# Layer 1's table, layer 2's scores and the shared outputs: an order of work changed at three places of a four-layer kernel

## The chip, the core and the metric

The kernel runs on one core of a Trainium2 chip. The core has TensorE (PE, matrix products and turns through an identity), VectorE (DVE), ScalarE (ACT), GpSimd (POOL, which here also issues the indirect DMAs) and SyncE (SP, which issues plain DMAs). Each engine takes its own instructions strictly in the order of the program's list for it and waits for the others by semaphores. The metric is the time of one execution on the device, in microseconds; shown is the median of three runs.

## What is computed

2048 tokens (8 sequences of 256) of 512 numbers pass four layers. Each layer adds a gated attention-like part and a gated feed-forward part to the tokens x, both of the normalised tokens. The change touches the seam of layers 1 and 2 and layer 2 with layer 3's attention beside it. Cut to that:

```python
# layer 1, feed-forward: 64 experts, 8 chosen for each token, and a shared one
out1 = experts(x, topk_idx, topk_w) + (silu(x @ sh_gate) * (x @ sh_up)) @ sh_down
x = x + tanh(g_ffn[1]) * out1

# layer 2, attention over channels, for each sequence
scaled = einsum('bsd,bse->bde', q, k) / sqrt(512)      # q = layernorm(x), k = v = ctx
out = einsum('bde,bse->bsd', softmax(scaled, axis=1), v)

# layer 2, feed-forward
out2 = gelu(x @ proj1.T + b1) @ proj2.T + b2

# layer 3, attention: a recurrence over the 256 tokens of a sequence, channel by channel
def step(carry, kv_t):                                 # k = layernorm(x), v = ctx
    aa, bb, pp = carry
    q = max(pp, u + kt)
    y_t = (exp(pp - q) * aa + exp(u + kt - q) * vt) / (exp(pp - q) * bb + exp(u + kt - q))
    q2 = max(pp + w, kt)
    return (exp(pp+w-q2) * aa + exp(kt-q2) * vt, exp(pp+w-q2) * bb + exp(kt-q2), q2), y_t

# layer 3, feed-forward: 8 experts, 2 chosen for each token, and a shared one
```

## The kernel before

All numbers are float32. The tokens stay in 16 tiles `xt[0..15]` of 128 tokens; four tiles make a block of 512 tokens (`NB` = 4 blocks), two a sequence. The program is a list written by hand in Python, and a list scheduler orders each engine's instructions by their place in the program and by a model of when their inputs are ready. `behind(one, other, reason)` adds a pure order constraint: `one` stands after `other` in the list. `with tc.high_priority` moves work forward in it. Where work of two kinds is to be interleaved, one of them is a Python generator, and the other calls `step` or `next`, which places the generator's next piece at this point. Matrix products go to four PSUM banks `mm`, turns to two banks `tr`, and two banks `ac` take the rest.

**Layer 1.** `attend1(blk, step)` (from L833) computes the attention of a block, and each of its calls of `step(n)` does two things (L1145): it advances `work()`, which routes the pairs of tiles q = 0 to 6 one after the other through `route1(q)` (from L969), and it issues up to `n` of the pending table writes. With `hurry` both are done twice; the second sequence of the last block is attended with `hurry` (L861). A table write (L950) is an indirect DMA from POOL that puts 128 choices, one from each token of a tile, into their experts' rows of a table in device memory; there are 16 to a route, 128 in all, and each may be told to come after a given product of PE. `route1(q)` normalises (statistics and `ve` on DVE, `rstd` on POOL at L166, `xn` on DVE), turns and scores its two tiles, chooses experts on DVE, and finds the weight of each choice with 16 small DVE operations `hit` (L1064).

After the attention the last route, q = 7, runs at high priority beside the shared expert of blocks 0 to 2. `shared1(blk)` (L1087) has five pieces: the products shg, shu and shr, with a multiplication `shT` on DVE in two parts at L1110, and two pieces of down products shd (16 PE passes for a block), each of which is scaled and added to its tiles of `xt` on DVE at L221. The loop at L1162 takes a piece of `shared1`, writes up to three pending choices behind the piece's last product, and takes a piece of `route1(7)`; in the eighth round that gives `order`, the experts by how many tokens they have, from which SP loads expert weights. All 16 choices of route 7 are written without such a tie. Then the table is read back (`rows`, L1177, one indirect DMA after all 128 writes), turned by PE into `who_ps` (L1193), and copied as `who` (DVE) and `share` (ACT). `who` is what the experts' tiles gather their tokens by (`xg`, L1213), on POOL; `tr_xg` turns what was gathered. The experts add their results by indirect DMA to two copies of the output in device memory, `acc`.

Last, after the experts, come the shared expert of block 3 (L1336), and `combine` (L1344), which loads the two copies of a tile (`more`, through eight buffers `t2`, by SP) and adds them to `xt` on DVE, L1352.

**Layer 2.** `back()` combines and normalises block 0 by pairs of tiles (L1725), and so lets the scores of the first sequence begin. `xattn2(blk)` (L1369) has for each of two sequences four score products `s` of PE, each followed by a maximum (L1385), an exponential `E` on ACT (L1387), a reciprocal and a scaling of `vs` (L1391); then four outputs `o`. The keys `kxvs` are loaded by SP, into a pool `bp` of five buffers that also holds one of the two `E` and, for layer 3, the turned tokens `xnT_a` and the exponents `ex`. `ready2` places the norm for the feed-forward part, `ffn2`, beside the second sequence; `ffn2` (L1436) has four quarters of four first products `h2p` (a gelu on ACT behind each) and four second ones `o2f` (a DVE addition behind each). Its weights `p` come by SP through seven buffers `wp`.

**Layer 3 beside it.** `tail(blk)` (L1681) is layer 3's attention and routing of a block: one piece for the norm, 12 for each of four groups of 128 channels (scans `pp`, `aa`, `bb`, and `q`, `ex`, `num`, `den` and a reciprocal on DVE; differences and products on POOL; an exponential on ACT), then four pauses, four pieces that turn and add the result, and nine of routing, of which the last ones issue eight table writes from POOL (L1669): 66 in all. It is advanced by `step(n, behind)` (L1699) of the back part; `held` puts the first DVE operation of a piece behind the given instruction. `tail(0)` and `tail(1)` are spread over `xattn2(2)`, `ffn2(1)` and over `xattn2(3)`, `ffn2(2)`; `tail(2)` over `ffn2(3)`; `last(blk, i)` (L1709) flushes what is left with `step(1000)` after the first `o2f` of the last quarter.

## Time and profile before

| | |
|---|---|
| time, three runs | 2718.54, 2718.95, 2723.67 us; median 2718.95 |
| the profiled execution | 2704.81 us, of which the span from first to last instruction is 2703.0 |
| PE busy | 2553.9 us, 94% of the span |
| DVE, ACT, POOL busy | 1288.3, 671.9 and 890.6 us (48, 25 and 33%) |
| mean granted TensorE clock | 0.974 |
| DMA | 333.04 MB moved, mean 123 GB/s |

The page gives, besides such totals, the span in 40 equal slices of 67.6 us, with one digit for each, the busy share in tenths (PEclk is the clock that TensorE was granted, in tenths of its full speed):

```profile
PE   7889898999999899999999899898999999999998
DVE  7656575536655622222222641767666674121121
PEclk9999899999999899999999999999999999999999
```

Layer 1's attention ends at 912 us, in the fourteenth slice; its experts run from 984 to 1494; layer 2 begins at 1518, in the 23rd slice, and ends at 2141; from there on it is layer 3's feed-forward part. DVE is nearly full where layer 2 begins and has room while its feed-forward part runs. Further views show single instructions in order of time, what each engine waited for, and busy times of a stretch. In them a line reads: start, duration, engine, line of the program, operation, output<-inputs, shape, number of instructions, and in brackets how long the engine had been idle before and what ended that.

### The profile page before, as it was taken

To read this page: it belongs to the slowest core of one execution; us is meant where nothing else is said; L and a number is where in the kernel's file an instruction comes from. 1 tells how busy PE (TensorE), PEld (TensorE's weight loads), DVE (VectorE), ACT (ScalarE), POOL (GpSimd) and SP (SyncE) were. 2 spreads that over 40 slices of the span, in tenths; PEclk is the share of its full clock that TensorE was granted. 3 is DMA by queue.
4 is the path that set the end of the run, shared out by engine and by line. 5 is a ranking of instruction groups with operands and counts; after the bars stand their busy time and mean duration, and the time that the engine had idled before them with its cause. 6 is when DMAs were issued, how large, how long until landed. Compare 5 with 4: busy or idle time off the path is not lost. (4 is left out here: it accounts for less than half of the span.)

```text
span 2703.0 us, 29475 instructions
## 1 busy us (share of the span) xinstructions
PE 2553.9 (94%) x10253; PEld 1355.1 (50%) x10268; DVE 1288.3 (48%) x3535; ACT 671.9 (25%) x1505; POOL 890.6 (33%) x814
## 2 busy tenths in 40 slices
PE   7889898999999899999999899898999999999998
PEld 3445444455665445555555344344454444455554
DVE  7656575536655622222222641767666674121121
ACT  2534344311111113333333211222223231111110
POOL 1111110112444445656565110333333342333332
PEclk9999899999999899999999999999999999999999
DMA  5000000112200259999997721132121211888884
GB/s 214 9 16 24 20 36 4 33 36 63 64 25 25 59 175 237 246 242 246 243 241 169 224 113 64 38 110 61 61 91 67 106 16 47 278 276 270 288 278 113
DMA packets 96187, 333.04 MB, mean 123 GB/s; under 512 B 20608, under 2 KB 23041, under 8 KB 88098
## 3 DMA queue, kind: packets, MB, share of 16 engines
q0 software_dynamic: 45856, 156.51, 23.0%
q1 hardware_dynamic: 47154, 170.34, 18.6%
q10 hardware_dynamic: 3024, 4.25, 0.5%
q8 instruction: 84, 1.38, 0.2%
q14 instruction: 69, 0.57, 0.1%
HBM read 280.46 MB, written 64.91 MB: 128 GB/s over the span
## 5 line engine op out<-in xcount | busy, mean ns | idle before, releaser
L210 PE MATMUL gu<-w,eb 128*128 128x352 f32 x896 | 285.9, 462 | 0.0
L1293 POOL DMA_INDIRECT acc<-eb,who x112 | 177.5, 1585 | 175.5 <-DVE eb L102 148.3
L210 PE MATMUL h2p<-xnT_f,p 128*128 128x512 f32 x512 | 228.0, 601 | 3.0 <-ACT xnT_f L104 3.0
L210 PE MATMUL o2f<-p,h 128*128 128x512 f32 x512 | 224.8, 593 | 0.0
L210 PEld LDWEIGHTS gu<-w,eb 128*128 128x128 f32 x896 | 162.6, 192 | 73.4 <-issue 2.3
L950 POOL DMA_INDIRECT table<-pay,rowi x128 | 126.1, 985 | 120.6 <-issue 26.1
L539 ACT ACTIVATE pr<-pr,n 128x256 f32<-128x256 f32 x256 | 127.9, 501 | 151.7 <-DVE n L534 148.8
L210 PEld LDWEIGHTS h2p<-xnT_f,p 128*128 128x128 f32 x512 | 97.2, 192 | 120.8 <-issue 115.7
L210 PEld LDWEIGHTS o2f<-p,h 128*128 128x128 f32 x512 | 96.2, 190 | 117.4 <-issue 115.2
L1213 POOL DMA_INDIRECT xg<-xnd,who x112 | 117.2, 1046 | 59.6 <-PE ehp L1240 22.8
L221 DVE SCALAR_TENSOR_TENSOR x<-o2f,tg,x 128x512 f32<-128x512 f32 x64 | 47.0, 739 | 140.7 <-PE o2f L210 140.7
L1768 PE MATMUL g_r<-w,xgT 128*128 128x352 f32 x288 | 111.7, 469 | 0.7 <-ACT xgT L104 0.7
L1768 PE MATMUL u_r<-w,xgT 128*128 128x352 f32 x288 | 108.7, 459 | 0.0
L1284 PE MATMUL ed<-w,eb 128*128 128x512 f32 x224 | 105.7, 594 | 0.9 <-DVE eb L1241 0.9
L102 DVE COPY eb<-ed 128x512 f32<-128x512 f32 x56 | 38.7, 692 | 138.6 <-PE ed L1284 138.6
L1775 DVE SCALAR_TENSOR_TENSOR h_r<-a_r,share,u_r 128x352 f32<-128x352 f32 x36 | 20.9, 581 | 175.9 <-PE u_r L1768 167.4
L1791 PE MATMUL d_r<-w,hT_r 128*128 128x512 f32 (+1 forms) x216 | 104.2, 592 | 0.0
L534 DVE CUSTOM_DVE_ANT_0 pr<-s,mask 128x256 f32<-128x256 f32 x256 | 96.9, 417 | 12.2 <-PE s L514 8.8
L1230 DVE SCALAR_TENSOR_TENSOR eb<-eb,share,gu 128x176 f32<-128x176 f32 x112 | 44.0, 393 | 122.0 <-ACT eb L1229 122.0
L591 POOL TENSOR_TENSOR y<-y,gbo 128x512 f32<-128x512 f32 x16 | 20.4, 1272 | 246.8 <-DVE y L590 239.0
L188 PEld LDWEIGHTS tr_xg<-ident,xg 128*128 128x128 f32 x592 | 68.9, 141 | 63.2 <-issue 49.9
L188 PE MATMUL tr_xg<-ident,xg 128*128 128x128 f32 x592 | 92.7, 280 | 6.4 <-DMA xg<-xnd,who 6.3
(534 smaller groups left out, 4730.5 us busy)
## 6 DMA issues: line engine op xcount, KB each, us to landing
w<-in_w SPq DMA_DIRECT2D x64, 960.0 KB, 7.3
p<-in_p SPq DMA_DIRECT2D x64, 512.0 KB, 5.7
xnd<-xn_f SPq DMA_DIRECT2D x32, 256.0 KB, 3.2
acc<-xnd SPq DMA_DIRECT2D x32, 256.0 KB, 4.9
more<-acc SPq DMA_DIRECT2D x32, 256.0 KB, 4.3
wd<-in_wd SPq DMA_DIRECT2D x64, 96.0 KB, 6.9
ctxTa<-in_ctxT SPq DMA_DIRECT2D x4, 1024.0 KB, 6.0
x<-in_x SPq DMA_DIRECT2D x16, 256.0 KB, 5.9
```

Source lines behind the costliest of these rows:

```text
L188: one = nc.tensor.transpose(ps[:, k, :], src[:, ts(k, P)], ident)
L210: one = nc.tensor.matmul(ps, lhsT[k], rhs[k], start=(k == 0), stop=(k == n - 1))
L221: return nc.vector.scalar_tensor_tensor(xt[i], ps, scale, xt[i], ALU.mult, ALU.add)
L534: one = nc.vector.tensor_tensor_reduce(pr[:, nt, :], ps[r][:, nt, :], mask[:, nt, :], -1.0, -LOW, ALU.add, ALU.min, n16[:, nt, h : h + 1],)
L539: nc.scalar.activation(pr[:, nt, :], pr[:, nt, :], AF.Exp, bias=n16[:, nt, h : h + 1], scale=-1.0, accum_out=s16[:, nt, h : h + 1],)
L950: one = nc.gpsimd.indirect_dma_start(out=table[:, :], out_offset=bass.IndirectOffsetOnAxis(ap=rows, axis=0), in_=choice, in_offset=None, b ...
L1213: nc.gpsimd.indirect_dma_start(out=xg, out_offset=None, in_=xnd[:, :], in_offset=bass.IndirectOffsetOnAxis(ap=who[:, c : c + 1], axis=0), ...
L1230: nc.vector.scalar_tensor_tensor(self.h, self.h, share[:, c : c + 1], gu[:, I1 : 2 * I1], ALU.mult, ALU.mult)
L1284: one = nc.tensor.matmul(ps[n], t.hT[rows, k, :], wd, start=(k == 0), stop=(k == 1))
L1293: nc.gpsimd.indirect_dma_start(out=acc[n][:, :], out_offset=bass.IndirectOffsetOnAxis(ap=who[:, t.c : t.c + 1], axis=0), in_=t.x, in_offse ...
L1768: nc.tensor.matmul(ps[:, 0:I3], xTt[:, k, :], wgu[k][:, g, :], start=(k == 0), stop=(k == KC - 1))
L1791: one = nc.tensor.matmul(ps, hT[:cn, n, :], wd[n][:cn], start=(n == 0), stop=(n == 2))
```

## The change

It is a set of small reorderings:

1. In the second sequence of layer 1's last block the last four calls of `step` advance the routing but write no choices (`quiet`). Their writes stay pending and are issued by later calls.
2. In `route1` the first `hit` stands behind the latest shared multiplication `shT` (`hidden`).
3. The loop of shared pieces ends two pieces earlier, 13 instead of 15. The rest of route 7, the table's read, `who_ps`, `who` and `share` come next, and then the last two pieces, the down products of block 2. The first of them is put behind the second turn of `who_ps` (`turned`). `who` is put behind the last shared multiplication rather than behind the last addition; the shared additions lose their fixed place.
4. The shared outputs of block 3 (`later`) are computed in two `ac` and two `mm` banks and are added to `xt[12..15]` only behind the last norm operation of layer 2's first two tiles.
5. `combine` adds on POOL instead of DVE for tiles 8 to 15.
6. `xattn2` calls `step` only at the first score of its first sequence, no longer at all eight; the four calls at the outputs stay. `ffn2` calls for three pieces at every `h2p`, also in its first quarter, where it called for two.

```diff
--- before.py
+++ after.py
@@ -166,6 +166,8 @@
         nc.gpsimd.tensor_tensor(out=rstd[:, :n], in0=ve[:, :n], in1=mhalf[:, :n], op=ALU.pow)
         yield ts_, mv, rstd
 
+    latest_norm = []
+
     def normed(stats, name, after=()):
         ts_, mv, rstd = stats
         out = []
@@ -175,6 +177,7 @@
             for other in after:
                 behind(one, other, "the scores first")
             out.append(xn)
+        latest_norm[:] = [one]
         return out
 
     def norm(blk, name):
@@ -858,7 +861,8 @@
                 for bb in range(BLK // S):
                     nm = f"{blk}_{bb}"
                     kf, V = context1(blk, bb, K, step) if bb else first
-                    if blk == NB - 1 and bb:
+                    quiet = blk == NB - 1 and bb
+                    if quiet:
                         step = lambda n: one_step(n, True)
                     qf = b8.tile([P, NH // 2, S], F32, tag="b8", name=f"qf_{nm}")
                     for cc in range(2):
@@ -929,13 +933,13 @@
                         aoT = t2.tile([P, KC, P], F32, tag="t2", name=f"aoT_{nm}_{nt}")
                         aoTs.append(aoT)
                         transpose4(aoT, aos[nt].rearrange("p h d -> p (h d)"), f"ao_{nm}_{nt}")
-                        step(1)
+                        step(0 if quiet else 1)
                     for nt in range(2):
                         ps = mmtile(f"wo1_{nm}_{nt}")
                         matmul_k(ps, [aoTs[nt][:, k, :] for k in range(KC)], [wo[:, k, :] for k in range(KC)])
                         i = blk * TB + bb * 2 + nt
                         add_scaled(i, ps, tg[:, 1:2])
-                        step(2 if nt == 0 else 0)
+                        step(0 if nt or quiet else 2)
                     done.append(blk * (BLK // S) + bb)
 
             tokens, done, counted = {}, [], []
@@ -1061,10 +1065,12 @@
                 hit = sm.tile([P, E1], F32, tag="hit", name=f"hit{q}", bufs=2)
                 for i in range(2):
                     for j in range(K1):
-                        nc.vector.scalar_tensor_tensor(
+                        one = nc.vector.scalar_tensor_tensor(
                             hit, key[:, i, :], key8[:, i, j : j + 1], w[:, i, :], ALU.is_equal, ALU.mult,
                             accum_out=pay[:, i, j, 1:2],
                         )
+                        if hidden and i + j == 0:
+                            behind(one, hidden[0], "the shared expert's first")
                     nc.vector.tensor_scalar(
                         pay[:, i, :, 1], pay[:, i, :, 1], den[:, i : i + 1], None, ALU.mult
                     )
@@ -1080,11 +1086,13 @@
                     ordered(expert)
                     yield
 
+            turned = []
+            hidden = []
             I1R = I1 - P
             rows_of = (slice(0, I1R), slice(FD, FD + I1R))
             rest1 = rows_of[1]
 
-            def shared1(blk, shgu):
+            def shared1(blk, shgu, later=None):
 
 
                 xnT = [tokens[blk][:, k, :] for k in range(KC)]
@@ -1110,10 +1118,11 @@
                     one = nc.vector.tensor_tensor(
                         pick(hT[1][rows_of[n], :]), pick(act[1][rest1, :]), pick(ps[rest1, :]), ALU.mult
                     )
-                last_add[:] = [one]
+                hidden[:] = [one]
                 yield
                 for i in range(0, TB, 2):
-                    ps = [mmtile(f"shd{blk}_{i + n}") for n in range(2)]
+                    bank, tag = (mm, "mm") if i or later is None else (ac, "ac")
+                    ps = [bank.tile([P, BLK], F32, tag=tag, name=f"shd{blk}_{i + n}") for n in range(2)]
                     last = None
                     for k in range(2):
                         for n in range(2):
@@ -1121,15 +1130,17 @@
                             one = nc.tensor.matmul(
                                 ps[n], hT[k][rows, ts(i + n, P)], shd[rows, k, :], start=(k == 0), stop=(k == 1)
                             )
+                            if turned:
+                                behind(one, turned.pop(), "the table's order first")
                             if last is not None:
                                 behind(one, last, "remainders side by side")
                             last = one
                     latest[:] = [last]
                     for n in range(2):
-                        one = add_scaled(blk * TB + i + n, ps[n], tg[:, 5:6])
-                        if i + n == 0:
-                            behind(one, last_add[0], "its place")
-                        last_add[:] = [one]
+                        if later is None:
+                            add_scaled(blk * TB + i + n, ps[n], tg[:, 5:6])
+                        else:
+                            later.append((blk * TB + i + n, ps[n], tg[:, 5:6]))
                     yield
 
             def work():
@@ -1139,7 +1150,6 @@
                         yield
                     yield from route1(q)
 
-            last_add = []
             gen = work()
 
             def step(n, hurry=False):
@@ -1159,7 +1169,8 @@
                 one = route1(2 * NB - 1)
                 for _ in range(3):
                     next(one)
-            while next(two, 0) is None:
+            for _ in range(5 * (NB - 1) - 2):
+                next(two)
                 write(3, latest[0])
                 with tc.high_priority(offset=400):
                     next(one, 0)
@@ -1193,11 +1204,14 @@
                 one = nc.tensor.transpose(who_ps[:, n, :], rows[:, :, n], ident)
                 if n == 0:
                     behind(one, latest[0], "the table comes late")
+            turned.append(one)
             who = l2.tile([P, P], I32, tag="who", name="who")
             one = nc.vector.tensor_copy(who, who_ps[:, 0, :])
-            behind(one, last_add[0], "the table comes late")
+            behind(one, hidden[0], "the table comes late")
             share = l2.tile([P, P], F32, tag="share", name="share")
             nc.scalar.copy(share, who_ps[:, 1, :])
+            for _ in two:
+                pass
 
             class Tile:
 
@@ -1333,10 +1347,10 @@
             with tc.If(some > PAIRS1):
                 experts1([(PAIRS1 + E1 + 2 * n, False, (wpool, "w")) for n in range((E1 - PAIRS1) // 2)])
 
-            end = shared1(NB - 1, again)
+            end = shared1(NB - 1, again, last_adds)
             for _ in range(3):
                 next(end)
-            first_loads.append(combine(range(2), adds=last_add))
+            first_loads.append(combine(range(2), adds=hidden))
             for _ in end:
                 pass
 
@@ -1349,13 +1363,13 @@
                 one = nc.sync.dma_start(more, results[u][ts(t, P), :])
                 for other in after:
                     behind(one, other, "not before it in the queue")
-                add = nc.vector.tensor_tensor(xt[t], xt[t], more, ALU.add)
+                add = (nc.vector if t < 2 * TB else nc.gpsimd).tensor_tensor(out=xt[t], in0=xt[t], in1=more, op=ALU.add)
                 if adds:
                     behind(add, adds[0], "its place")
                     adds[:] = [add]
         return one
 
-    kxvs, kx_load, first_loads = {}, [], []
+    kxvs, kx_load, first_loads, last_adds = {}, [], [], []
 
     def load_kx(b, b8, after=None):
         t = b8.tile([P, 4 * C], F32, tag="b8", name=f"kxvs{b}")
@@ -1394,7 +1408,8 @@
                 if bb:
                     latest_dve[:] = [one]
                     next(ready, None)
-                step(1, one)
+                elif ec == 0:
+                    step(1, one)
         for bb, (vs, E) in enumerate(parts):
             b = blk * (BLK // S) + bb
             for nt in range(2):
@@ -1450,7 +1465,7 @@
                 ps = mmtile(f"h2p_{q}_{blk}_{j}")
                 matmul_k(ps, [p1[:, k, :] for k in range(KC)], [xT[:, k, :] for k in range(KC)])
                 one = nc.scalar.activation(h[:, j, :], ps, AF.Gelu, bias=b1[:, c : c + 1])
-                step(2 if q < 1 else 3, one)
+                step(3, one)
             for i in range(TB):
                 ps = mmtile(f"o2f_{q}_{blk}_{i}")
                 matmul_k(ps, [h[:, j, ts(i, P)] for j in range(KC)], p2)
@@ -1727,6 +1742,10 @@
                 loaded = combine(tiles, kx_load) if bb else first_loads.pop()
                 kxvs[bb] = load_kx(bb, bp, loaded)
                 xns += norm_of(tiles, f"a2{bb}_")
+                other = latest_norm[0]
+                for add in last_adds:
+                    behind(add_scaled(*add), other, "layer 2's first tokens first")
+                last_adds.clear()
             context(0, loaded)
             first_loads.append(loaded)
             emptied()
```

## The prediction

> **What bounds the kernel now.** I read the page first: PE is busy 94% of the span, so time can only come from PE's idle stretches and from its slow ones, where the PEclk digits fall. The page's chain of waits holds only the last 2 us and gives nothing. So I asked for PE's waits in the two stretches that the change touches (columns: us in total, times, longest), here 900 to 990 us, the end of layer 1's attention:
>
> ```profile
> PE tr_xg L188 <- DMA xg<-xnd,who: 6.3, 1, 6.3
> PE tr_f L188 <- DVE xn_f L174: 5.3, 1, 5.3
> PE shd L1121 <- DVE shT L1110: 3.4, 1, 3.4
> ```
>
> and 1500 to 1910 us, from layer 1's last shared products into layer 2:
>
> ```profile
> PE s L210 <- DMA kxvs<-in_ctx: 8.0, 2, 6.1
> PE o L210 <- ACT E L1387: 6.0, 2, 5.7
> PE s L210 <- DVE xn_a__0_12283 L174: 5.2, 1, 5.2
> PE tr_f L188 <- DVE xnT_f L102: 4.5, 2, 2.4
> ```
>
> Seven kinds of wait, 38.7 us. Then the busy times by stretch (PE, PEld, DVE, ACT, POOL, granted clock, DMA share, GB/s):
>
> ```profile
> 905.00:990.00 85.00, 69.94 (x176) 31.31 (x175) 33.57 (x144) 9.12 (x13) 38.99 (x40) 0.84 0.35 113
> 1535.00:1581.00 46.00, 43.35 (x113) 19.80 (x112) 42.92 (x108) 9.61 (x24) 8.96 (x7) 1.00 0.56 207
> 1690.00:1735.00 45.00, 35.44 (x99) 16.62 (x98) 37.30 (x76) 10.48 (x21) 15.00 (x14) 0.91 0.14 53
> 1854.00:1900.00 46.00, 36.36 (x100) 17.07 (x99) 38.66 (x76) 10.49 (x21) 15.92 (x15) 0.90 0.28 56
> ```
>
> The reader sees that the waits bring a second loss: the clock is 0.84 to 0.91 where PE stalls and 1.00 where it doesn't. Its size comes from the same products after a wait and without one: 32 h2p products 15.63 against 14.00 us, 24 o products 12.56 against 10.46, 16 s products 9.06 against 7.03, the first gathered tiles 3.1 too long, the products after the 5.3 and 3.4 us waits 2.4 and some 4.3.
>
> Last, the order of time around the table:
>
> ```profile
> 914.49 0.97 POOL L950 DMA_INDIRECT table<-pay,rowi  x1 [0.30 <-issue]
> 915.48 0.75 POOL L166 TENSOR_TENSOR rstd_f<-ve_f,mhalf 128x2 f32<-128x2 f32 x1
> ...
> 957.75 0.97 POOL L950 DMA_INDIRECT table<-pay,rowi  x1 [0.30 <-issue]
> 964.76 1.02 POOL L1177 DMA_INDIRECT rows<-table,row_c  x1 [6.03 <-DMA table<-pay,rowi]
> 977.01 0.51 PE L1193 MATMUL who_ps<-ident,rows 128*128 128x128 f32 x2
> 978.99 1.03 POOL L1213 DMA_INDIRECT xg<-xnd,who  x1 [13.21 <-DMA wd<-in_wd]
> 983.86 1.97 PE L188 MATMUL tr_xg<-ident,xg 128*128 128x128 f32 x8 [6.34 <-DMA xg<-xnd,who]
> ```
>
> rstd_f stands behind eight table writes; `who_ps` is turned 12 us after its read was issued, because PE has block 2's products in front of it.
>
> **Part A, the table.** (1) `quiet` takes eight writes (steps of 1, 1 and 2, doubled by the hurry) from before route 7. ve_f was done at 911.0; with POOL free rstd_f follows at 911.3, xn_f at 912.1, PE at 912.7: a wait of 1.1 instead of 5.3. The writes are not gone: 16 instead of 8 now meet the loop's `write(3, latest[0])`, which also wait for PE. (2) The hits behind the shared product let the two shT products (0.42 each) pass some eight hits of 0.34: the 3.4 us wait becomes some 0.8. (3) What decides is now POOL's queue. From the end of shg, some 914.8, it has 32 writes at 1.28 us and one 1.5 us pause for shu: the last ends at 957, where it ended at 958.7. That write landed 6.0 us later, beside four weight loads that `order` released at 955; a write's median landing is 2.1. With (1) and (2) `order` comes some 13 us earlier and those loads are through, so I take 3.5 (bounds 2.1 and 6.0). The read then starts at 960.7, its rows land 2.8 after its 1.02, and who_ps is turned at about 965 instead of 977.0. PE gets there at 977.0 - 13.5 (less waiting, full clock) - 5.9 (the moved products) = 957.6 and **waits 7.4 us with nothing behind it that may pass**: all 16 shd passes are pinned behind it. A new wait, then. After it: 0.9 us of turning, 5.9 of products, 2.5 for the clock; tr_xg at 974.3. The gather needs 1.5 + 4.9 us from who_ps, until 971.4, hidden by the products; without that cover it would cost its 6.3 again. Before, 983.9 + 3.1 for the clock = 987.0. **Saved 12.7**; with who_ps at 963 and 2.0 for the clock 15, at 968.6 and 4.3 only 7.3. who's cast moves on DVE and its copy on ACT, both idle there; the gathers' POOL queue is empty, SP's order is unchanged.
>
> [...] The rows say more: after 2.40, then 1.1 of transposes and 0.81, the h2p products still lost 1.6. [...] I take the rows.
>
> **Part B, layer 2's first tokens.** Of the DVE work in front of xn_a__0, four shd adds of 0.75 leave, three of them (2.06 us) after the last product: chain of four 0.68 adds, two statistics, rstd and xn puts xn_a at 1514.0 instead of 1516.7, PE at 1514.7 instead of 1517.7, and the slow clock behind it (2.45) may go too. But DVE stays full (25.0 of 28 us in that stretch) and gets the same adds a little later, so the second pair's xn stays at 1524.4; PE, done with the first at 1521.6, waits. What remains is s of the second pair at 1524.7 instead of 1527.0: 2.3. The held banks are free by 1517.1 and needed at 1518.1: nothing, 3 us if that cover goes. The 16 adds of blocks 2 and 3 leave DVE (0.68 each, 10.9 us) for POOL, idle from 1544.6 to 1569; the copies' buffers return sooner, so SP issues the kxvs load behind them earlier and its 2.0 us wait goes. **Saved 4.3**, bounds 1 and 8.
>
> [...] Rows of 1690 to 1735 agree that it isn't free:
>
> ```profile
> L174 DVE TENSOR_SCALAR xn_f<-x,mv_f,rstd_f 128x512 f32<-128x512 f32 x4 | 3.8, 1018 | 0.8 <-POOL rstd_f L166 0.8
> L174 DVE TENSOR_SCALAR xn_a<-x,mv_a,rstd_a 128x512 f32<-128x512 f32 x4 | 2.1, 536 | 0.1
> ```
>
> xn_f ran beside POOL's adds, xn_a didn't. [...] By the row twelve DVE operations slow by up to 0.5 us: DVE keeps 5 of its 10.9, enough for the 2.0.
>
> **Part C, the recurrence.** In 1690 to 1735 DVE does q, ex, aa, bb, num and den between the scores; these rows of it show the cost:
>
> ```profile
> 1704.45 1.86 DVE L1499 SCALAR_TENSOR_TENSOR ex<-xnT_a,tf,q 128x512 f32<-128x512 f32 x1
> ...
> 1711.22 0.67 DVE L1385 TENSOR_REDUCE m<-s 128x1 f32<-128x512 f32 x1
> 1711.92 0.15 DVE L1386 TENSOR_SCALAR m<-m 128x1 f32<-128x1 f32 x1
> ```
>
> The maximum that frees a bank for o starts 3.9 us after the last score, behind a scan that waited for POOL. With one step left on the scores it starts at once, as in 1535 to 1581, where the same work ran without recurrence and o never waited for E. Saved: 5.7, 2.1 (o), 2.0 of 2.4 (a 0.74 ex still comes before the copy) and 1.6 (h2p): 11.4. In 1854 to 1900 PE waits 6.1 for kxvs, issued behind four p loads at 1854.74 and landed 15.4 later: that has nothing to do with the recurrence and stays. Saved there 1.7 + 1.7 = 3.4. The moved steps (aa, bb, num, den, reciprocal: 9.4 us of DVE) lie beside ffn2's products, where DVE was busy 76.9 of 119 us. **Saved 14.8**, bounds 8 and 24. In block 2's tail four more steps come before the flush: its 1.0 us wait at 2127 may go, **1.0**.
>
> **Sum**: 12.7 + 4.3 + 14.8 + 1.0 = 32.8 us from the profiled execution, 2704.8 us with a span of 2703.0. The median shown, 2718.95, is 14 above it; I take the saving in us from it: 2686.
>
> **Rivals.** *The wait comes back* (0.25): rows land no earlier than the read's 968.6, the clock costs 4.3 more, the second pair is as late as ever: 7.3 + 2.0 + 14.8 = 24, time 2695. For it: POOL's queue is as long as before. *More falls* (0.14): kxvs's buffer is asked for before the first ex now, so its load may go ahead of the p loads; 6.1 + 2.0 more, 2678. Against it: SP keeps its order. *The recurrence doesn't move* (0.10): the steps are only floors and the program's order is a list; DVE takes the work as soon as it is ready: C gives nothing, 2701; should POOL's later writes take A's gain as well, no change. *Backlog* (0.07), the slower side: the tail has 66 steps, and exactly 66 calls stand before the flush where 69 stood. If DVE falls behind by one channel (some 15 us alone, 22 beside POOL by the xn rows), it stands in front of the next norm in two blocks: 2 x (22 + 2.5) = 49, 2735. It decides once DVE's 76.9 + 9.4 us exceed the stage's 110, which they don't.
>
> **Numbers.** The forecast itself has 0.44, with its own range 2678 to 2695. Low end 2674: *more falls* with A at 15. High end 2706: A 7.3 and C halved. Left out is the backlog and some 0.1 at the edges. Under 0.2% (5.4 us) nothing can be told from no change. Faster 0.89, within 0.04, slower 0.07.
>
> **What would show it.** PE waits some 7 us for rows in front of who_ps and not for xg after it; rstd_f follows ve_f at once; o no longer waits for E; clock in 1690 to 1735 near 1.00; kxvs still awaited once. It is wrong if who_ps is turned after 970, if a table write stands before a norm's rstd at a block's start, or if o2f begins to wait.

## The result, and the profile after

The changed kernel takes 2740.84 us (median of six runs, 2730.47 to 2744.68), the kernel before beside it 2721.19 (six runs, 2718.54 to 2724.47): a ratio of 1.0068, 95% interval 1.0049 to 1.0087. It is **slower by some 19 us**, where 33 us less were forecast. The profiled execution took 2730.47 us, with a span of 2728.7 against 2703.0 and a mean clock of 0.973 against 0.974.

The slices of the page (one digit for each fortieth of the span, 68.2 us here), to be laid beside those of before:

```profile
PE   7889898999999989999999899998999899999997
DVE  7656575536655722222222631766667475111121
PEclk9999999999999989999999999999999899999999
```

Two clock digits have fallen that were 9: the fifteenth slice (955 to 1023 us, the table) and the 32nd (2115 to 2183, the end of block 2's recurrence). The waits of PE in the same two stretches as before (us in total, times, longest) say what stands there. First 900 to 1000 us:

```profile
PE shg L213 <- DVE x L224: 4.5, 1, 4.5
PE tr_xg L191 <- DMA xg<-xnd,who: 3.5, 1, 3.5
PE shr L213 <- DVE x L224: 2.1, 1, 2.1
PE tr_f L191 <- DVE xn_f L176: 0.9, 1, 0.9
PE shd L1130 <- DVE shT L1118: 0.8, 1, 0.8
```

The waits for `xn_f` and for `shT` have shrunk as forecast, from 5.3 and 3.4 us. New are two waits for the addition of a shared product, 6.6 us together, and the gather is still awaited. Then 1500 to 1910 us:

```profile
PE s L213 <- DMA kxvs<-in_ctx: 9.3, 2, 5.7
PE h2p L213 <- ACT xnT_f L104: 4.8, 3, 2.0
PE tr_f L191 <- DVE xnT_f L102: 3.9, 2, 2.5
...
PE s L213 <- DVE xn_a__0_12279 L176: 2.4, 1, 2.4
...
PE o2f L213 <- ACT h L1467: 1.2, 1, 1.2
```

`o` waits for `E` no longer, and the wait for the first tokens has halved. But `h2p` now waits up to 2.0 us for `xnT_f`, and `o2f` waits for a gelu, which no row of before did. Last the busy times of the three stretches of before (PE, PEld, DVE, ACT, POOL, clock, DMA share, GB/s); the same work lies 12, 14.4 and 10 us later here:

```profile
917.00:1002.00 85.00, 72.67 (x205) 32.46 (x204) 39.70 (x177) 9.70 (x14) 42.82 (x44) 0.91 0.38 122
1704.40:1749.40 45.00, 39.83 (x109) 18.67 (x108) 35.98 (x76) 11.31 (x22) 15.37 (x14) 0.92 0.14 53
1864.00:1910.00 46.00, 35.12 (x99) 16.63 (x98) 30.75 (x69) 10.32 (x21) 16.99 (x16) 0.90 0.29 56
```

In block 2's scores (the middle row) PE went from 35.4 to 39.8 us of 45, but the clock only from 0.91 to 0.92. PE's rows there, before and after, say why:

```profile
1713.00 12.56 PE L210 MATMUL o<-E,kxvs 128*128 128x512 f32 x24 [5.66 <-ACT E L1387]
...
1732.27 1.09 PE L188 MATMUL tr_f<-ident,xn_f 128*128 128x128 f32 x8 [2.40 <-DVE xnT_f L102]
1734.18 15.63 PE L210 MATMUL h2p<-xnT_f,p 128*128 128x512 f32 x32 [0.81 <-ACT xnT_f L104]
```

```profile
1721.56 10.46 PE L213 MATMUL o<-E,kxvs 128*128 128x512 f32 x24
...
1738.78 1.09 PE L191 MATMUL tr_f<-ident,xn_f 128*128 128x128 f32 x8 [2.45 <-DVE xnT_f L102]
1741.90 16.77 PE L213 MATMUL h2p<-xnT_f,p 128*128 128x512 f32 x32 [2.03 <-ACT xnT_f L104]
```

The wait for `E` and the slow `o` products behind it are gone, as forecast; the waits in front of `h2p` are not, and `h2p` has become slower. Half of the forecast gain has come true there. The loss is elsewhere. The table cuts the span at instructions of PE that all kernels share; the third column is a later profile of the kernel before (e5 below), the fourth the best version (e10 below):

| stretch of PE's work, us | before | after | before again | best |
|---|---|---|---|---|
| layer 1's attention, `kf` at 648 us to the first count | 282.4 | 294.5 | 310.3 | 275.7 |
| the table, to the first `tr_xg` | 53.2 | 54.8 | 52.4 | 49.0 |
| layer 1's experts | 510.6 | 510.6 | 510.9 | 509.6 |
| shared outputs, to the first `s` | 23.2 | 20.4 | 23.2 | 24.4 |
| `xattn2` of blocks 0 and 1 | 62.8 | 66.5 | 63.3 | 63.2 |
| `xattn2` of block 2, to its first `h2p` | 43.7 | 37.0 | 43.7 | 37.0 |
| `ffn2` of block 1 | 119.9 | 122.2 | 124.2 | 124.7 |
| `xattn2` of block 3 | 43.7 | 44.7 | 44.3 | 39.8 |
| `ffn2` of block 2 | 122.7 | 125.0 | 121.5 | 127.7 |
| `ffn2` of block 3, to layer 3's first `sg` | 124.7 | 137.0 | 124.8 | 124.6 |

Where columns one and two differ, the 25.7 us between the two spans are these: layer 1's attention 12.1, the last `ffn2` 12.3, the two before it 4.6, the first `xattn2` row 3.7, the table 1.6 and block 3's `xattn2` 1.0, against 6.7 and 2.9 saved (stretches left out differ by 0.1). The change does not touch layer 1's attention until its last block, and the third column shows the kernel before itself with more of that loss: the first pair of profiles can't be subtracted as it stands.

### The profile page after: what moved, and what is told of

Read it like the earlier page. It is cut to its first block, busy times and chain, and to the rows that moved or that the text cites. A ratio compares the mean times of both kernels' runs of the same rounds, so it can differ in the third digit from the quotient of the medians.

```text
span 2728.7 us, 29479 instructions
## 1 busy us (share of the span) xinstructions
PE 2567.2 (94%) x10268; PEld 1358.4 (50%) x10268; DVE 1284.2 (47%) x3519; ACT 668.4 (24%) x1503; POOL 913.5 (33%) x830
## 5 line engine op out<-in xcount | busy, mean ns | idle before, releaser
L542 ACT ACTIVATE pr<-pr,n 128x256 f32<-128x256 f32 x256 | 127.9, 501 | 151.0 <-DVE n L537 148.1
L537 DVE CUSTOM_DVE_ANT_0 pr<-s,mask 128x256 f32<-128x256 f32 x256 | 96.7, 416 | 12.3 <-PE s L517 8.6
L213 PE MATMUL sg<-xnT_f,shgu 128*128 128x512 f32 x192 | 90.5, 611 | 10.2 <-DMA shgu<-in_shgu 10.2
L1467 ACT ACTIVATE h<-h2p,b 128x512 f32<-128x512 f32 x64 | 43.5, 687 | 227.8 <-PE h2p L213 227.7
```

Source lines behind the costliest of these rows:

```text
L213: one = nc.tensor.matmul(ps, lhsT[k], rhs[k], start=(k == 0), stop=(k == n - 1))
L537: one = nc.vector.tensor_tensor_reduce(pr[:, nt, :], ps[r][:, nt, :], mask[:, nt, :], -1.0, -LOW, ALU.add, ALU.min, n16[:, nt, h : h + 1],)
L542: nc.scalar.activation(pr[:, nt, :], pr[:, nt, :], AF.Exp, bias=n16[:, nt, h : h + 1], scale=-1.0, accum_out=s16[:, nt, h : h + 1],)
L1467: one = nc.scalar.activation(h[:, j, :], ps, AF.Gelu, bias=b1[:, c : c + 1])
```

## Experiments

All ratios are to the kernel before on the same chip in the same set of runs, with a 95% interval. There were five sets. In the first, second and fourth the kernel before took about 2728 us, in the third and fifth about 2704. So a difference in us counts within its set only.

**First set: which part costs the time?** The change once more (e1), the recurrence alone (e2), all but the recurrence (e3), the table alone (e4: items 1 to 3 of the change, except that the shared additions keep their fixed place, and without items 4 to 6).

```diff
 # e2: before, with
-                step(1, one)
+                elif ec == 0:
+                    step(1, one)
-                step(2 if q < 1 else 3, one)
+                step(3, one)
 # e3: after, with the lines of before put back at these places
```

e1, the change:

> The changed kernel once more, nothing altered. Its first profile loses some 16 us against before's between 694 and 925 us, in layer 1's attention, where TensorE's order of instructions is still the same as before: five of the kf groups of 64 products, 2.01 us in one piece before, come in pieces with 0.3 us pauses put down to issue. Theory 'the execution': these pauses belong to that one execution. Then kf runs whole again here, lgp_f of block 3 starts near 916 instead of 933, and the 11 us in which DVE's adds and the second half of block 2's shared products stood still at 963 to 982 are gone too. Theory 'the program': the pauses come again at the same products, and the span is again near 2728. Time by both: 2730 to 2745, 1.005 to 1.009 of before.

e2, the recurrence alone:

> Before with the recurrence alone changed: no step on the scores but at the first context chunk, three steps on each product of the first quarter too. Theory 'recurrence costs': in the profile of the changed kernel it won 6.7 us at block 2's scores and lost 2.2 in block 0's tail, 1.3 in block 1's, some 12 in block 2's (gelus late behind the recurrence's exponential, the last norm later, the shared weights awaited) : sum +8 to +12 us, 1.003 to 1.0045. Theory of the prediction (part C): -14.8 us, 0.9945. Theory 'table costs': near the prediction's.

e3, without the recurrence:

> The changed kernel with the recurrence's steps put back on the scores and two per product in the first quarter. Theory 'recurrence costs': all of the loss is the recurrence's, so this is 8 to 12 us under the changed kernel, 2729 to 2733, or lower where the table helps as predicted (12.7 + 4.3 us under before, 2702). Theory 'table costs': 2750 or more, as the recurrence's gain is taken away.

e4, the table alone:

> Before with the table's order alone changed: no table writes in the last batch's attention, hits behind the shared product, who_ps turned ahead of block 2's last sixteen shared products. The shared outputs of block 3 and the adds of the combine are as before. Theory of the prediction (part A): -12.7 us, 0.9953; bounds -7 to -15. Theory 'table costs': the writes, which now run until the expert weights' loads have begun, and the stall seen at 963 to 982 come with it: +5 to +11 us.

Measured: e1 1.0055 [1.0039, 1.0071], e2 1.0057 [1.0037, 1.0078], e3 0.9994 [0.9984, 1.0003], e4 0.9989 [0.9979, 0.9999]. **The recurrence alone is the whole loss**, some 16 us of 2728; the table gains 3 us, and the shared outputs with `combine`'s additions on POOL (e3 against e4) nothing that can be told.

**Second set: which half of the recurrence?** The kernel before, profiled once more (e5); the steps off the scores, with two steps in the first quarter as before (e6, the first edit of e2); three steps in the first quarter, with the scores as before (e7, its second edit); and e6 with two steps behind each `o2f` of the second quarter, which brings the calls before the flush of blocks 0 and 1 back from 62 to 66 (e8; before has 69).

```diff
 # e8: e6, with
-                step(1, one)
+                step(2 if q == 1 and blk < NB - 1 else 1, one)   # behind an o2f
```

e5:

> The kernel before once more, for a second profile. All four profiles so far other than its first show the kf groups of layer 1 in pieces, also the one that changes the recurrence alone and has layer 1 unaltered. Theory: the first profile of before was an execution without these pauses, and its usual one has them: kf in pieces here, lgp_f of block 3 near 938 us instead of 920, span 2715 to 2730. Otherwise (the pauses belong to the changed programs): kf whole at 2.01 us, span near 2703.

e6:

> Before with the recurrence's steps off the scores alone, two per product in the first quarter as before. Theory 'phase of the exponential': a channel has 12 pieces, its exponential is the 4th, and on ACT it costs two table loads and itself, 4.5 us; in block 2's tail, which no scores precede, nothing moves, so the 12 us lost there by the changed kernel don't come; blocks 0 and 1 win the 6 to 7 us of the wait for E and lose 1 to 2 each where the exponential now falls on the third product of a quarter: -3 to -9 us, 0.997 to 0.999. Theory 'DVE is short of time': work that leaves the scores is missing later, the next norms come late: as bad as the recurrence's whole change, +10 to +18 us.

e7:

> Before with three steps on each product of the first quarter instead of two, the scores as before. Theory 'phase': in block 2's tail the exponential of the last channel moves from the third quarter's second half onto its third product, as in the changed kernel, the last gelu waits some 4 us, block 2's end comes later and the shared weights are awaited: +8 to +13 us, 1.003 to 1.005; blocks 0 and 1 lose nothing. Theory 'DVE is short of time': earlier steps help, 0 to -3 us.

e8:

> The scores alone, and in blocks before the last two steps on each output tile of the second quarter, so that the last channel's exponential falls on the second product of the third quarter and not on its third, and as many steps stand before the flush as there are pieces. Theory 'phase': 1 to 3 us better than the scores alone: -6 to -11 us, 0.996 to 0.998. Theory 'DVE is short of time': like the scores alone.

Measured: e6 1.0052 [1.0032, 1.0073], e7 1.0078 [1.0060, 1.0096], e8 1.0039 [1.0027, 1.0051]; e5 took 2734.11 us with a span of 2732.4. Each half loses by itself, and each in its own place. In e7 it is the end of block 2's recurrence, which runs in the last `ffn2`. POOL's order of time there, before (first two lines of eight table writes, and the rstd of layer 3's next norm):

```profile
2143.46 1.01 POOL L166 TENSOR_TENSOR rstd_a<-ve_a,mhalf 128x4 f32<-128x4 f32 x1 [15.79 <-DVE ve_a L164]
2147.80 1.04 POOL L1669 DMA_INDIRECT table<-pay,row  x1 [3.33 <-DVE hit L1661]
2149.15 0.97 POOL L1669 DMA_INDIRECT table<-pay,row  x1 [0.30 <-issue]
```

and in e7 (the first and last of the eight writes):

```profile
2186.08 1.04 POOL L1669 DMA_INDIRECT table<-pay,row  x1 [22.07 <-DVE hit L1661]
...
2195.01 0.95 POOL L1669 DMA_INDIRECT table<-pay,row  x1 [0.30 <-issue]
2195.99 1.04 POOL L166 TENSOR_TENSOR rstd_a<-ve_a,mhalf 128x4 f32<-128x4 f32 x1
```

The order has turned. Counted from the kernels, block 2's tail, which has no scores beside it, gets 57 of its 66 pieces placed before the flush in before and 61 in e7: none of the nine pieces of routing, and four of them. The writes, in the last two pieces, come with the flush both times, but with four pieces of routing placed earlier the list has them in front of `rstd_a`, which now starts 10 us after the first of them. (How the scheduler's model arrives at this order no run shows.) The loads of layer 3's shared weights meet the same writes. PE's wait for them, in before and in the changed kernel:

```profile
2145.18 3.78 PE L210 MATMUL sg<-xnT_f,shgu 128*128 128x512 f32 x4 [1.25 <-DMA shgu<-in_shgu]
```

```profile
2170.75 2.08 PE L213 MATMUL sg<-xnT_f,shgu 128*128 128x512 f32 x2 [7.12 <-DMA shgu<-in_shgu]
```

The loads are issued at the end of the last `o2f` in both. In before the first `sg` starts 4.3 us after the issue (2140.93), here 7.1 (2163.66), with the first write 0.8 us ahead of the loads. The other profiles divide in the same way: in e1, e2, e7, e13 and the changed kernel, with three steps in the first quarter, it takes 6.9 to 7.5 us; in all others, where the writes follow, 4.0 to 4.5.

In e6 that end is in order, and the loss stands one and two blocks earlier. The eight writes of block 1's tail run from 2043.37 to 2053.3, `ve_a` of the next norm was done at 2044.9, and `rstd_a` starts only at 2053.29, 8.4 us late; in block 0's tail it is 8.6 (1880.31 to 1888.88). DVE and PE in e6 (the two engines in order of time; PE's `tr_a` turns what DVE's `xn_a` gives):

```profile
2054.37 1.92 DVE L174 TENSOR_SCALAR xn_a<-x,mv_a,rstd_a 128x512 f32<-128x512 f32 x4 [9.46 <-POOL rstd_a L166]
```

```profile
2055.06 1.94 PE L188 MATMUL tr_a<-ident,xn_a 128*128 128x128 f32 x8 [6.68 <-DVE xn_a L174]
```

The steps that left the scores were not only work on DVE, they were places in the list. With fewer calls before the flush the routing at a tail's end comes later: in PE's order its products `pos` stand 16 product groups ahead of the end of block 1's `ffn2` in e9 below, 13 in before, 8 or 9 in e2 and e8, 2 in e6. The writes follow them by 3 us, take 10, and reach into the next block's norm. The delay of `rstd_a` follows the number of calls: 8.6 and 8.4 us with 62 calls (e6), 4.2 and 2.6 with 66 (e8), 0.1 with 69 or 70 (before and e9). So e8, which was to gain on the theory that the exponential's place alone counts, loses too. In the changed kernel, with 66 calls in blocks 0 and 1 and 61 in block 2, both happen: `tr_a` waits 1.81 us at 2039.29, `sg` 7.12 at 2170.75.

A third cost can be seen in the changed kernel. ACT in order of time (table load, the recurrence's exponential, table load, gelu), and PE behind it:

```profile
2110.91 1.28 ACT L1520 ACT_TABLE_LOAD   x1 [5.97 <-DVE ex L1514]
2112.20 1.91 ACT L1520 ACTIVATE ex<-ex 128x2048 f32<-128x2048 f32 x1
2114.13 1.28 ACT L1467 ACT_TABLE_LOAD   x1
2115.42 0.69 ACT L1467 ACTIVATE h<-h2p,b 128x512 f32<-128x512 f32 x1
```

```profile
2116.16 11.38 PE L213 MATMUL o2f<-p,h 128*128 128x512 f32 x22 [4.23 <-ACT h L1467]
```

An exponential and its two table loads hold ACT for 4.5 us. Between the earlier gelus of a quarter that is hidden behind the products (in before, with exponentials at 2081.98 and 2102.14, PE is busy 30.00 of the 30 us from 2077 to 2107); here the new count of steps has put it in front of the last gelu, which all the rest of `o2f` waits for. This happens four times in the changed kernel (1.2, 1.2, 0.7 and 4.2 us), 7.3 us in all. Of the 12.3 us of the last `ffn2`, the waits in it explain 10.0 (1.8 for `tr_a`, 5.0 for `h`, 7.1 for the weights, the rest 1.7, against 5.6 in all before); of what is left, 2.3, the 22 passes above lose 1.8: 11.38 us, where 22 passes of this shape take 9.61 in before without a wait (the clock is 0.90 from 2111 to 2128 us).

**Third set: give the places back.** If the missing places are the cause, calls elsewhere should take the loss away. e9 is e6 with two steps behind the `o2f` of two quarters (70 calls); e10 adds the table of e4 to it. e11 and e12 vary the table without the recurrence: e11 holds all expert weights of SP behind the table's read, e12 leaves out `quiet`.

```diff
 # e9, e10
+                step(2 if q in (1, 2) and blk < NB - 1 else 1, one)   # behind an o2f
 # e11: e4, with
-... weight(..., ahead=c < 4)
+... weight(..., ahead=False)
```

e9:

> The recurrence off the scores as in the change, two steps per product in the first quarter as before, and in blocks before the last two steps on each output tile of the second and the third quarter: 70 calls before the flush where before had 69 and the change 66. In TensorE's order the routing's counting product then stands 16 product groups (0.86 us each) ahead of the end of block 1's feed-forward; before 13, the change 8 to 9, the scores alone 2. Theory 'table writes before the next rstd': eight writes of 1.28 us begin 3 us behind that product and must be through before rstd_a of the next norm, so 15 us of distance are wanted: here no wait for xn_a, block 2's tail as before, only the gain of the scores stays: -5 to -8 us, 0.997 to 0.998. Theory 'DVE is short of time' or 'the exponential's phase alone': like the run with 66 calls, +8 to +11 us, 1.003 to 1.004.

e10:

> The table's order of the change with the recurrence evened as in the run before this one. If the two stages are independent: -3 (measured for the table) and -5 to -8: 0.996 to 0.997. If not: no better than the better of the two.

e11:

> The table's order of the change, and the first experts' weights are not loaded before the table's read is issued (in the other kernels the first loads start at the ranks' order, beside the last table writes). In the profiles of the table's order DVE's first shared add of block 1 comes 12 to 18 us late, at the end of the last write, and TensorE's next product waits 5 to 7 us. Theory 'loads beside writes': without loads beside them DVE's add follows its product, shg doesn't wait, who_ps comes at the rows' landing; the first experts' weights come later instead, some 0 to 6 us: 0.995 to 0.999. Theory 'the writes alone' or 'code loading': DVE's add is as late as before and the weights cost on top: 1.000 to 1.003.

e12:

> The table's order of the change without its first part: the last batch's eight table writes stay in front of route 7's norm (24 writes behind it and not 32), hits behind the shared product and who_ps turned early as in the change. Theory 'the queue of writes decides': TensorE waits 5.3 us for xn_f again and loses 2.4 more to the clock, but the last write comes up to 10 us nearer to the ranks' order, and the stall of DVE and TensorE in front of the last write (12 and 7 us) shrinks by as much: 0.997 to 0.999, not worse than with the quiet part. Theory 'quiet is the gain': 1.000 to 1.002.

Measured: e9 0.9995 [0.9986, 1.0005], e10 0.9959 [0.9946, 0.9972], e11 0.9960 [0.9947, 0.9973], e12 0.9966 [0.9954, 0.9978]. The loss is gone in e9, and with it both waits: the last `ffn2` takes 124.6 us as before, and block 2's scores keep their 37.0. Yet nothing is won. The waits of PE in e10, 1560 to 2145 us:

```profile
PE h2p L210 <- ACT xnT_f L104: 4.5, 4, 2.0
...
PE o2f L210 <- ACT h L1465: 3.5, 2, 1.8
PE y L1556 <- POOL xnT_a L1546: 2.4, 2, 1.2
```

Twice 1.8 us for an exponential in front of a gelu and twice 1.2 for POOL's last product of a channel: 3.0 us in each of the first two `ffn2`, which take 4.8 and 5.0 us longer than in before, what the scores had saved. The 22 passes of `o2f` behind each wait of 1.8 take 9.71 us, where 22 take 9.61 without one; in the second `ffn2` the 32 `h2p` products behind a wait of 2.04 us take 16.96, 1.3 more than in before; the rest is not accounted for. (For the first of them the measure is rough: the two profiles of the kernel before differ there by 4.3 us.)

The table is another matter here. All three forms gain 0.34 to 0.41% (9 to 11 us), and PE's waits in e10, 900 to 985 us, are of the kinds that the prediction drew, with a shorter wait for rows (7.4 forecast) and one for the gather (none forecast):

```profile
PE tr_xg L188 <- DMA xg<-xnd,who: 3.5, 2, 3.1
PE who_ps L1202 <- DMA rows<-table,row_c: 2.4, 1, 2.4
PE tr_f L188 <- DVE xn_f L174: 0.9, 1, 0.9
PE shd L1127 <- DVE shT L1115: 0.8, 1, 0.8
```

**Why did the table gain 3 us in one set and 11 in another?** In e4, from DVE and POOL in order of time:

```profile
972.33 0.88 DVE L1115 TENSOR_TENSOR shT<-sha,shr 48x256 f32<-48x256 f32 x2
985.42 0.75 DVE L221 SCALAR_TENSOR_TENSOR x<-shd,tg,x 128x512 f32<-128x512 f32 x1 [12.22 <-remote]
```

```profile
984.40 0.97 POOL L951 DMA_INDIRECT table<-pay,rowi  x1 [0.30 <-issue]
987.42 1.02 POOL L1186 DMA_INDIRECT rows<-table,row_c  x1 [2.04 <-issue]
```

DVE has its inputs (PE's `shd` ended at 979) and stands still until POOL has issued its last write; the trace has no semaphore for it, only "remote". PE's `shg` then waits 7.2 us for this addition. Every profile with the table's new order shows this stop in the first and fourth sets and in the changed kernel's first profile (there 8.0 us, which PE pays with the 4.5 and 2.1 above), and none in the third and fifth; with the old order no profile has it. Wherever the stop can be seen, and in the same sets with the old order too, PE pauses inside layer 1's smallest products: 13 or 14 times in each of twelve profiles, always in the same five groups of `kf`, and never in the eight others. One of `kf`'s groups of 64 in before, and one in e5, the same kernel:

```profile
694.99 2.01 PE L798 MATMUL kf<-WkfT,K 32*128 32x64 f32 x64
```

```profile
695.58 1.57 PE L798 MATMUL kf<-WkfT,K 32*128 32x64 f32 x45
697.45 0.45 PE L798 MATMUL kf<-WkfT,K 32*128 32x64 f32 x4 [0.30 <-issue]
698.20 0.45 PE L798 MATMUL kf<-WkfT,K 32*128 32x64 f32 x3 [0.30 <-issue]
698.94 0.68 PE L798 MATMUL kf<-WkfT,K 32*128 32x64 f32 x12 [0.29 <-issue]
```

The pauses are small, but the clock in 840 to 905 us is 0.89 in e5 against 1.00 in before, and layer 1's attention takes 310 us instead of 282. So the first profile of before came from an execution without pauses, and that of the change from one with them.

**Fourth set: does holding the loads remove that stop, and is a fuller first `o2f` better?** The change a third time (e13); e10 with three steps behind the `o2f` of one quarter (e14); that with e11's held loads (e15).

e13:

> The changed kernel, a third time. On the chips of the first and second group of runs TensorE paused in kf and DVE stood still behind the ranks' order; in the third group no kernel did, before ran 2704 us and the table's order won 9 to 12 us. If the loss is the recurrence's (table writes before rstd in block 1's and block 2's tail, the last gelu behind the exponential): its stages cost 12 to 16 us net here too, f3 to sg 137 or more. On a chip without pauses: table -11, recurrence +15: 1.001 to 1.003. With pauses: 1.005 to 1.008.

e14:

> The table's order with the evened recurrence, the eight moved steps all on the second quarter's output tiles (three each), so that the last channel's exponential is done before the third quarter's gelus. Without that exponential among the gelus (1.8 us of waits in each of two blocks, a wait of 1.2 for the last channel, and the clock behind them): 3 to 6 us better than the evened form, 0.994 to 0.996 on a chip without pauses, 0.997 to 0.999 with them. If the phase isn't it: as the evened form, 0.996.

e15:

> As the run before this one, and the experts' weights held behind the table's read. On a chip with pauses: theory 'loads beside writes' has DVE's first shared add of block 1 within 3 us of its product and 0 to 7 us won against the run before; theory 'code loading or writes alone' has it 10 us late as before, time equal or some us longer. On a chip without pauses both: equal within 0.1%.

Measured: e13 1.0075 [1.0049, 1.0101], e14 1.0041 [1.0024, 1.0058], e15 1.0026 [1.0012, 1.0040]. This set had the pauses (before 2728.70). Three steps at once overshoot: `y` waits for POOL's `xnT_a` 7.5 us, twice. In e15 DVE still stands for 10.5 us with the loads held, so it isn't the weight loads beside the writes that stop it.

**Fifth set: is it a matter of the place in the list?** The best version again (e16); the table with 64 small clears on DVE ahead of layer 1, to move all its later instructions (e17); the kernel before with 32 small products on PE there (e18).

```diff
 # e17                                       # e18
+for _ in range(64):                         +for _ in range(32):
+    nc.vector.memset(spare, 0.0)            +    nc.tensor.matmul(ps[:, 0:2], ident, ident[:, 0:2], ...)
```

e16:

> The table's order with the evened recurrence (two steps on the tiles of the second and third quarter) again, for a second chip. Without pauses in kf: 0.996 as measured. With pauses the table's 11 us shrink to 3 and the recurrence's part stays at 0: 0.998 to 1.000.

e17:

> The table's order alone with 64 small clears on VectorE ahead of layer 1 (some 4 us of DVE in which it is half idle), which move everything behind them 64 instructions on in DVE's stream. On a chip with pauses, theory 'place in the stream': DVE's stall of 10 to 18 us at block 1's shared adds goes from there to another place, and the time changes by more than 3 us one way or the other. Theory 'state of the queues': the stall stays at the same adds, ends with the last table write as before, and the time is that of the table's order, 0.999 to 1.001.

e18:

> The kernel before with 32 small products on TensorE ahead of layer 1 (64 records, some 2 to 4 us), which move everything behind them 128 instructions on in TensorE's stream. The pauses in kf so far come every 520 to 545 instructions (counted at 7092, 7632, 8174, 8695 and 9241 of loads and products together). [...] Theory 'kf itself': kf is in pieces at the same products, +2 to +4 us.

Measured: e16 0.9955 [0.9941, 0.9969], e17 0.9962 [0.9949, 0.9976], e18 1.0049 [1.0033, 1.0065]. No profile of this set shows a pause of `kf` or a stop of DVE, so the question that e17 and e18 were made for stayed unanswered; e17 gave one more measurement of the table without pauses, and e18 a surprise told below.

## Why the prediction was wrong

**The step that failed** is in part C and in the rival called *backlog*: the moved steps were counted as DVE work that "lie beside ffn2's products", and the 66 calls against 69 were weighed by DVE's load alone ("it decides once DVE's 76.9 + 9.4 us exceed the stage's 110, which they don't"). DVE was not short of time: in the first two `ffn2` of the changed kernel it is busy 82.6 of 122 and 86.1 of 125 us. A call that is taken away or added moves every later piece in the list, POOL's eight table writes and ACT's exponential with them, and those met a norm's `rstd`, a weight load and a last gelu. The prediction named two signs of it, "a table write stands before a norm's rstd at a block's start" and "if o2f begins to wait"; both came. It gave 0.07 to a mechanism of this place and took its price from the wrong engine; and it entered block 2's tail as a gain.

Point by point, by the stretches of the first pair:

- **Block 2's scores**, forecast 11.4: 6.7. The 5.7 for `E` and the 2.1 of the `o` products behind it went in full. The 2.0 before `tr_f` did not: it still waits 2.45, and `h2p` behind it 2.03 instead of 0.81. The 1.6 of the `h2p` products turned into a loss of 1.1 (16.77 us after 15.63), which the row of the next `ffn2` holds. A clock "near 1.00" between 1690 and 1735 was named as a sign; in the changed kernel these times hold earlier work and show 1.00, but over the same work the clock is 0.92.
- **Block 3's**, forecast 3.4: 1.0 lost. `kxvs` stayed the last to arrive, as forecast (5.7 us after 6.1), and `tr_f` waits 1.4 instead of 2.1. Against this `tr_a` waits 1.0 for `xn_a`, whose `rstd_a` stands behind block 0's table writes (its input was done at 1866.16, it starts at 1870.40), and `h2p` waits 2.0 instead of 0.8.
- **Moved steps**, forecast 0: 2.2 and 2.4 lost in the first two `ffn2`, of which 1.2 and 1.2 are waits for a gelu; the rest is no more than before's own two profiles differ there (4.3 and 1.2).
- **Block 2's tail**, forecast 1.0 gained: 12.3 lost. The 1.0 us wait for `xn_f` is there unchanged; the four earlier pieces turned POOL's order instead. This term and its sign made the result; with the recurrence alone the runs give 16 us of loss where 15.8 of gain were forecast.
- **The table**, forecast 12.7. From `kf` at 648 to the first `tr_xg` before took 335.6 us and e10, e11 and e17 324.7, 323.9 and 323.7: 11 to 12 us, and 9 to 11 by the ratios of the sets without pauses. `rstd_f` and `shT` came true to 0.2 us or better. The wait for rows was 2.4 (e10) to 5.3 us (e17) instead of 7.4, and the gather, which was to be hidden, still cost 1.7 to 3.5: errors that cancel. In the sets with pauses DVE's stop (12.2 us in e4, for which PE waits 7.2) takes most of it: 3 us are left (e4).
- **First tokens**, forecast 2.3: 2.9. **The additions on POOL**, forecast 2.0: 3.7 lost, so that part B is nought; of it 0.9 lies in the first sequence's scores, where the gain of the first tokens shrinks from 2.9 to 2.0. POOL needs 1.32 us for an addition (14.57 for 11) and DVE 0.68, so the buffers of the copies come back later, not sooner. SP waits 11.1 us for POOL between 1536 and 1575, its `kxvs` load behind them is issued 4.5 us after block 1's first score instead of 3.0, and PE's wait for it is 3.6 instead of 2.0, with 1.7 more in the products behind it. The additions were never moved alone, so this cause is read from the rows, not tested.
- **The clock.** The prediction took the loss behind short waits from the rows, and the rows were right again: behind gaps of 2.45 and 2.03 us, with a turn of 1.1 between, the 32 `h2p` products of block 2 took 16.77 us against 14.00 without a wait, at a clock of 0.83 (0.89 over the 15.63 us of the same products in before).
- **The range.** Its ends don't follow from the terms named for them: these come to 2676 and 2699, where 2674 and 2706 stand. Nothing hangs on it, as the time lies above both.

What is shown: the recurrence is the loss (e2, e3); each half loses alone (e6, e7); calls given back elsewhere remove it (e9). The loss was measured in sets with pauses and e9 in one without, so these ratios alone would not do. The stretches tell the two apart: without three steps in the first quarter and with the scores' steps kept, the last `ffn2` takes 124.5 to 126.2 us in sets of both kinds, in the changed kernel and in e2 137.0 to 141.4, and in e9 124.6. (e14 and e15, with 70 calls in a set with pauses, have `rstd_a` in time as well; they take 127.9 and 128.0 there and lose the rest to the waits for `xnT_a`.) That the writes' place is the main cause rests on the order in all profiles and on the delay of `rstd_a` with 62, 66 and 70 calls. Moving the writes alone was not tried, and the exponential's place moved with them, so their shares stay open. What stops DVE beside POOL's last writes in some sets stays open too, and so does what makes the pauses. It is not the chip alone: the first set, with pauses, and the third, without, ran on the one numbered 15 both times.

The best version, e10 and its repeat e16 at 0.9959 and 0.9955, beats the kernel before where it was measured (2690 to 2692 us against 2704); the changed kernel was not run in those two sets. It is not told apart there from the table's order without the recurrence (e11 with held loads and e17 with 64 clears: 0.9960, 0.9962), and it was not run in a set with pauses. The part worth keeping is the table.

## What to carry to other kernels

In a list with interleaved generators a call is a place and not only a piece of work: when a change removes calls, count the calls up to the next flush, write down where every engine's last pieces land, the indirect DMA issues (here one every 1.28 us) and table loads (1.28 us each) of other engines among them, and look at which norm, load or last activation stands there. Price the engine that those pieces end on, not the one that was to be relieved. And profile the unchanged kernel twice before subtracting two profiles: here its own two spans differed by 29 us, more than the effect.

## What the runs showed of the hardware that was not expected

- The same kernel ran at 2704 and at 2728 us in different sets. In the slower ones PE's products of 31 ns (`kf`) break off for 0.3 us at a time, thirteen times between 690 and 1000 us in e5 (4.1 us), and the clock is 0.89 from 840 to 905 us, where it was 1.00 without them. What breaks them off no run shows.
- 32 products of two columns (64 passes in the trace) took 10.87 us in e18, 0.17 for a pass where `kf`'s 64 passes of 64 columns take 2.01 in all; the `kf` group behind them took 3.69, where the same group takes 2.01 in before, and the kernel was 13 us slower. PE had no gap in these 10.87 us, and yet the `kf` group ran, by these two times, at some 0.54 of its rate in before (an estimate). The mean clock of the profiled execution is 0.972, that of before in the same set 0.975. So two columns instead of 64 did not make a product cheaper here, and a stream of such products, though PE counts as busy, did not keep the products behind it at their speed.
- The shared weights reached their first use 4.0 to 4.5 us after their issue where POOL's eight indirect writes of 128 rows each came later (fifteen profiles), and 6.9 to 7.5 where the first write came 0.8 us before them (five).
